# The preparation of a state-space scan, done by direction and half instead of by channel chunk

## The chip, the core and the metric

The kernel runs on one NeuronCore of a Trainium2 chip. The core has five engines that run side by side, each through its own list of instructions in order: TensorE (PE, matrix products, with its weight loads shown apart as PEld), VectorE (DVE, element by element), ScalarE (ACT, functions of one input), GpSimd (POOL, here two-input products), and SyncE (SP, which here issues most transfers). On-chip data lies in SBUF; matrix products land in PSUM[...]. The metric is the device time in microseconds (us) of one execution.

## What is computed

The input x has 8 images of 384 channels and 32 x 32 pixels, which are a sequence of L = 1024 places. Layer 0 normalizes it over the channels, runs a selective state-space model (Mamba) forward and backward over the sequence, adds a gated 3 x 3 depthwise convolution, and adds all to x. Layer 1 is a causal attention with 6 heads and a feed-forward part with sign weights and 8-bit scaling. The part that matters here, cut from the reference:

```python
xz = jnp.einsum('blc,ec->ble', x, in_proj_w)
u, z = jnp.split(xz, 2, axis=-1)
uc = conv_general_dilated(u...)                      # causal, 4 taps per channel
u = silu(uc + conv1d_b)
x_dbl = jnp.einsum('blc,ec->ble', u, x_proj_w)
dt, Bm, Cm = jnp.split(x_dbl, [dt_rank, dt_rank + D_STATE], axis=-1)
delta = softplus(einsum('blr,dr->bld', dt, dt_proj_w) + dt_proj_b)
h = exp(delta * A) * h + (delta * u) * Bm            # one step of the scan, 16 states
y = sum_n(h * Cm) + u * D_param
y = y * silu(z)
...
fwd = mamba(x_flat); bwd = flip(mamba(flip(x_flat)))
g = (fwd + bwd) * scale_mod
x = x + res_scale * (g + sigmoid(conv3x3(x_norm) + dw_b) * x_norm)
```

Everything is float32 except the causal mask. The forward and the backward scan use the same weights.

## The kernel before, in words

Channels lie on the 128 partitions, so C = 384 is three chunks c; places lie along a row, in two halves h of HB = 512 columns. The kernel is written as lists of small steps, each with an estimated weight in us. A scheduler orders the instructions that the steps record, and the tile pools decide which buffer each takes: `mid` has 10 buffers of 1024 columns, `big` 6 of 3 x 1024 columns, and PSUM has 8 banks (`da` 2, `s` 2, `pt` 2, `y` 1, `av` 1).

**The recurrence.** The scans of one batch are 96 units (`Unit`): four parts (direction d and half h, `PARTS` = forward first half, forward second, backward second, backward first), three chunks c, eight pairs of states n. A unit is: POOL multiplies `ud` (delta times u) by a broadcast row of B (`s_first`, L578); ACT makes exp(delta A) into PSUM (L591) and DVE scans, twice (L596, `s_scan`); POOL multiplies by a row of C (L602); PE transposes the product and adds it up in PSUM (L610, `s_sum`). After the last unit of a chunk and half, `s_gate` adds u D and multiplies by silu(z). A unit's first multiply is recorded two units ahead of its scan, and its loads (`ud`, `dl`, rows `bc`) four units ahead. The part's rows of B and C are read from DRAM.

**The preparation, `before_scan`.** It makes all of this for a batch ahead of its scans. It loads x, normalizes both halves (L330), and then goes by chunk: `in_proj` makes u (`up`) and z of both halves (L337, L344); `conv` makes the four-tap convolution for each direction and half, one tap on ACT (L353) and three on DVE (L363); `gates` applies Silu, makes the image convolution `local` (L374 and eight taps L384 on DVE), and spills x and z; the sum of the u of both directions (L428) and u itself go to DRAM. `project` multiplies u of the chunk by the x_proj weights; the chunks' contributions are added up in SBUF, in `xd`, by DVE (L488). After the third chunk, the rows of B and C are spilled and `delta` runs for every chunk, direction and half: it reloads u, one matmul (L508), four ACT functions (L511 to L514) and four DVE operations (L515 to L518), and spills delta (`dl`) and `ud`. [...]

**The order of the stages.** Batches go in the order 0, 1, 2, 3, 5, 6, 4, 7. The preparation of batch 0 runs first, but for its `gates` for z and the image (`later`). Then the first scans (`first`, the 96 units of batch 0) run with a list `beside` them: these gates, the preparations of batches 1, 2 and 3, and the binarization of the feed-forward weights. After that, the units of the next batch run beside the attention of the batch before (`attention`), and beside its feed-forward part (`feed_forward`, batches 0 to 4) together with the preparation of a batch three further on. The attention of the last batch has nothing beside it.

The steps are laid into one another by `spread_over`, in proportion to their weights; the lists are put together in these lines:

```python
before_scan(ORDER[0], ("s", "pt"), begin, beside)
run(begin)
beside += steps_of(before_scan, ORDER[1], ("s", "pt"))
...
run(first, beside)
```

Of the kernel before, what the change touches and what calls it, by code (L numbers as in the profile page):

```python
# [17 lines left out]
P = 128  # L18
# [35 lines left out]
def kernel(  # L54
# [251 lines left out]
    def before_scan(b, tags, emit, later=None):  # L306

        st = {}
        turns = itertools.cycle(tags)

# [3 lines left out]
        @emit  # L314
        def _():

            st["xn"] = btile(f"xn_{b}")
            load(st["xn"], x[b].rearrange("(c p) l -> p c l", p=P))
            st["xd"] = mtile(f"xd_{b}")

        for h in range(NH):

            @emit
            def _(h=h):
                sqs = squares(st["xn"], h, f"n0_{b}")
                ms = mean_of(lambda c: sqs[c], f"ms_{b}_{h}")
                rstd_of(ms, 0)
                for c in range(NC):
                    xc = st["xn"][:, c, half(h)]
                    nc.vector.scalar_tensor_tensor(  # L330
                        xc, xc, vec[:, c, V_NORM : V_NORM + 1], ms, ALU.mult, ALU.mult
                    )

        def in_proj(c, i, h):
            mp = bank_of(f"in_{b}_{c}_{i}_{h}")
            for k in range(NC):
                nc.tensor.matmul(  # L337
                    out=mp,
                    lhsT=st["win", c][:, k, i, :],
                    rhs=st["xn"][:, k, half(h)],  # L340
                    start=(k == 0),
                    stop=(k == NC - 1),
                )
            nc.scalar.copy(st["up" if i == 0 else "z", c][:, half(h)], mp)  # L344

        def conv(c, d, h):

            acc = bank_of(f"u{d}_{b}_{c}_{h}")
            up = st["up", c]
            for s in range(DCONV):  # L350
# [14 lines left out]
                st["u", d, c][:, half(h)], acc, AF.Identity, bias=vec[:, c, V_CB : V_CB + 1]  # L365
# [28 lines left out]
        def weights_of(c):  # L394
            w = mtile(f"win_{b}_{c}", NC * 2 * P).rearrange("p (k i e) -> p k i e", k=NC, i=2)
            for i in range(2):
                load(
                    w[:, :, i, :],
                    w_in[:, i * C + c * P : i * C + (c + 1) * P].rearrange("(k p) e -> p k e", p=P),
                )  # L400
            st["win", c] = w

        emit(lambda: weights_of(0))
        for c in range(NC):

            @emit
            def _(c=c):
                st["up", c] = mtile(f"up_{b}_{c}")
                st["z", c] = mtile(f"z_{b}_{c}")
                for d in range(2):  # L410
                    st["u", d, c] = mtile(f"u{d}_{b}_{c}")
                if c + 1 < NC:
                    weights_of(c + 1)

            for i in range(2):
                for h in range(NH):
                    emit(lambda c=c, i=i, h=h: in_proj(c, i, h), 2.6)
            for d in range(2):
                for h in range(NH):
                    emit(lambda c=c, d=d, h=h: conv(c, d, h), 3.0)  # L420

            def silus(ts):
                for t in ts:
                    pin(nc.scalar.activation(t, t, AF.Silu))

            def sum_of_us(c=c):
                usum = mtile(f"us_{b}_{c}")
                nc.vector.tensor_tensor(usum, st["u", 0, c], st["u", 1, c], ALU.add)  # L428
                spill((b, "us", c), usum, f"sus_{b}_{c}")
                for d in range(2):  # L430
                    spill((b, "u", d, c), st["u", d, c], f"su_{d}_{b}_{c}")


            def gates(c=c, silus=silus, sum_of_us=sum_of_us):
                st["xc"] = mtile(f"xc_{b}_{c}")
                load(st["xc"], x[b, chunk(c), :])
                accs = [local(c, h) for h in range(NH)]
                with tc.high_priority(offset=60):
                    us = [st["u", 0, c], st["u", 1, c]] if later is None else []
                    silus(us + [st["z", c]])  # L440
                    for h in range(NH):
                        pin(
                            nc.scalar.activation(
                                accs[h], accs[h], AF.Tanh, scale=0.5, bias=dwbh[:, c : c + 1]
                            )
                        )
                    pin(nc.scalar.preload_act_table_set(LOG_EXP))
                for h in range(NH):
                    acc, xc = accs[h], st["xc"][:, half(h)]
                    nc.vector.scalar_tensor_tensor(  # L450
                        acc, acc, 1.0, st["xn"][:, c, half(h)], ALU.add, ALU.mult
                    )
                    nc.vector.scalar_tensor_tensor(xc, acc, rsh, xc, ALU.mult, ALU.add)
                spill((b, "t", c), st["xc"], f"st_{b}_{c}")
                spill((b, "z", c), st["z", c], f"sz_{b}_{c}")
                if later is None:
                    sum_of_us()

            def gates_of_us(c=c, silus=silus, sum_of_us=sum_of_us):
                with tc.high_priority(offset=60):  # L460
                    silus([st["u", 0, c], st["u", 1, c]])
                    pin(nc.scalar.preload_act_table_set(LOG_EXP))
                sum_of_us()

            if later is None:
                emit(gates, 14.0)
            else:
                emit(gates_of_us, 4.0)
                later(gates, 10.0)


            for h in range(NH):

                def project(c=c, h=h):
                    xp = bank_of(f"xp_{b}_{c}_{h}")
                    for d in range(2):
                        nc.tensor.matmul(
                            out=xp[d * DW : (d + 1) * DW, :],
                            lhsT=wx[:, c, :],
                            rhs=st["u", d, c][:, half(h)],  # L480
                            start=True,
                            stop=True,
                        )
                    xd = st["xd"][:, half(h)]
                    if c == 0:
                        nc.scalar.activation(xd, xp, AF.Identity, bias=onerow)
                    else:
                        nc.vector.tensor_tensor(xd, xd, xp, ALU.add)  # L488

                emit(project)  # L490

        @emit
        def _():
            for d in range(2):
                rows = dram.tile([2 * NS, L], F32, name=f"rows{d}_{b}", tag=f"rows{d}")
                nc.sync.dma_start(out=rows, in_=st["xd"][d * DW + BC0 : (d + 1) * DW, :])
                spilled[b, "rows", d] = rows
# [3 lines left out]
        def delta(c, d, h):  # L501
            ew = mtile(f"ew{d}_{b}_{c}_{h}").rearrange("p (i l) -> p i l", i=2)
            du = mtile(f"du{d}_{b}_{c}_{h}").rearrange("p (i l) -> p i l", i=2)
            e, w, dl, u = ew[:, 0, :], ew[:, 1, :], du[:, 0, :], du[:, 1, :]
            load(u, spilled[b, "u", d, c][:, half(h)])
            dp = bank_of(f"dp{d}_{b}_{c}_{h}")
            r = slice(d * DW, d * DW + RANK + 1)
            nc.tensor.matmul(  # L508
                out=dp, lhsT=wdt[r, chunk(c)], rhs=st["xd"][r, half(h)], start=True, stop=True
# [6 lines left out]
            nc.vector.scalar_tensor_tensor(dp, w, 1.0, e, ALU.subtract, ALU.subtract)  # L516
            nc.vector.tensor_tensor(dl, dl, dp, ALU.subtract)
            nc.vector.tensor_tensor(u, u, dl, ALU.mult)  # L518
            for i, what in enumerate(("dl", "ud")):
                t = dram.tile([P, HB], F32, name=f"s{what}_{d}_{b}_{c}_{h}", tag=f"sp_{what}_{d}_{c}_{h}")  # L520
                nc.sync.dma_start(out=t, in_=du[:, i, :])
                spilled[b, what, d, c, h] = t

        for c in range(NC):
            for d, h in PARTS:
                emit(lambda c=c, d=d, h=h: delta(c, d, h), 3.0)
# [39 lines left out]
    def s_row(u, i):  # L566

        if not u.asks:
            return
        r = sp.tile([P, 2, HB], F32, name=f"bc{i}_{u.name}", tag=f"bc{i}", bufs=4)  # L570
        rows = spilled[u.b, "rows", u.d][i * NS + u.n : i * NS + u.n + 2, half(u.h)]
        load(r, rows.partition_broadcast(P))
        sst["bc", i, u.b, u.part, u.n] = r
# [57 lines left out]
    def s_gate(u):  # L631
# [6 lines left out]
        for what in ("us", "z"):  # L638
            t = sp.tile([P, HB], F32, name=f"{what}h_{u.name}", tag=what, bufs=1)
            load(t, spilled[b, what, c][:, half(h)])  # L640
# [451 lines left out]
    def steps_of(stage, *args):  # L1092
        out = Steps()
        stage(*args, out)
        return out
# [92 lines left out]
```

## Time and profile before

| | |
|---|---|
| time, median of 3 runs | 5227.8 us (5223.77 to 5229.38) |
| span of the profiled execution | 5226.4 us |
| PE busy | 4198.9 us (80%) |
| POOL busy | 3680.7 us (70%) |
| DVE busy | 3630.7 us (69%) |
| ACT busy | 2738.5 us (52%) |
| DMA, bytes moved | 696.35 MB, mean 133 GB/s |

How to read it: a busy engine is busy over the whole span on average, while the stages have different limits, so a stage must be looked at by itself. A group of instructions is named by line, engine, operation and tiles (out<-in); then come its count, its busy time, the mean of one in ns, the idle time of its engine just before it, and what ended that. The two multiplies of the recurrence, with their form:

```profile
L578 POOL TENSOR_TENSOR g<-ud,bc 128x1024 f32<-128x1024 f32 x768 | 1834.5, 2389 | 730.6 <-PE y L610 579.9
L602 POOL TENSOR_TENSOR g<-g,bc 128x1024 f32<-128x1024 f32 x768 | 1819.8, 2370 | 277.6 <-DVE g L596 215.5
```

They are 768 units of two multiplies of some 2.4 us, nearly all of POOL's work.

### The profile page before, as it was taken

The numbers are of one execution on the slowest core, as the hardware profiler recorded it, in microseconds if no ns is written. First come the engines' busy times: TensorE is split into PE (matmuls) and PEld (weight loads), VectorE is DVE, ScalarE is ACT, GpSimd is POOL, SyncE is SP. The second block draws the span as 40 slices with busy tenths as digits, with TensorE's granted clock in tenths as the row PEclk, the third lists the DMA queues.
The fourth block names the chain that finished last, engine by engine and source line by source line (L and its number), as shares of the span: only waits on it lengthen the run. The fifth ranks groups of instructions, "written<-read, shape, count | busy, mean of one in ns | idle before, by whom it ended". The sixth has DMA issues, their size and how long they took to land.

```text
span 5226.4 us, 50586 instructions
## 1 busy us (share of the span) xinstructions
PE 4198.9 (80%) x16554; PEld 2222.6 (43%) x16554; DVE 3630.7 (69%) x4313; ACT 2738.5 (52%) x4934; POOL 3680.7 (70%) x1932
## 2 busy tenths in 40 slices
PE   5455667888878888788887888978888888988799
PEld 2233333444434444444443444434444444544444
DVE  6998998667776667876677856678766655565522
ACT  4665564555644556545556445565464454463334
POOL 0477777887679776787776788677888877787600
PEclk7667677889988899888898889988999989999899
DMA  6544545324463234543244632335433234224200
GB/s 228 210 164 156 184 166 196 109 84 149 143 205 105 91 110 161 169 158 119 97 139 133 213 123 91 108 128 201 141 119 130 89 101 158 85 77 151 83 30 25
DMA packets 365007, 696.35 MB, mean 133 GB/s; under 512 B 30104, under 2 KB 88904, under 8 KB 364744
## 3 DMA queue, kind: packets, MB, share of 16 engines
q1 hardware_dynamic: 355232, 676.97, 38.3%
q10 hardware_dynamic: 9512, 16.15, 0.9%
q8 instruction: 131, 2.15, 0.2%
q14 instruction: 132, 1.08, 0.1%
HBM read 527.33 MB, written 165.68 MB: 133 GB/s over the span
## 4 chain that ended last, share of the span: by engine, by line
POOL 35%; PE 21%; issue 16%; DVE 15%; ACT 4%; DMA 1%; POOLq 0%; SPq 0%; DVEq 0%; ACTq 0%
POOL g L578 18%; POOL g L602 17%; DVE g L596 6%; PE y L610 3%; PE qp L715 3%; PE yp L1015 2%; PE av L854 2%; PE s L770 2%; PE ap L911 2%; DVE loc L384 2%; PE pt L842 1%; DVE dp L516 1%; DVE u L363 1%; PE hp L970 1%; DVE du L518 1%
## 5 line engine op out<-in xcount | busy, mean ns | idle before, releaser
L578 POOL TENSOR_TENSOR g<-ud,bc 128x1024 f32<-128x1024 f32 x768 | 1834.5, 2389 | 730.6 <-PE y L610 579.9
L602 POOL TENSOR_TENSOR g<-g,bc 128x1024 f32<-128x1024 f32 x768 | 1819.8, 2370 | 277.6 <-DVE g L596 215.5
L591 ACT ACTIVATE da<-dl,amat 128x512 f32<-128x512 f32 x1536 | 1057.5, 691 | 1572.1 <-DVE g L596 1530.2
L610 PE MATMUL y<-ident,g 128*128 128x128 f32 x6144 | 969.2, 307 | 403.1 <-POOL g L602 337.6
L596 DVE TENSOR_TENSOR_SCAN g<-da,carry,g 128x512 f32<-128x512 f32 x768 | 954.9, 1271 | 460.2 <-POOL g L578 413.2
L596 DVE TENSOR_TENSOR_SCAN g<-da,g 128x512 f32<-128x512 f32 x768 | 906.5, 1209 | 508.5 <-POOL g L578 483.0
L610 PEld LDWEIGHTS y<-ident,g 128*128 128x128 f32 x6144 | 798.8, 158 | 837.3 <-POOL g L602 504.1
L770 PE MATMUL s<-k,q 64*128 64x512 f32 (+3 forms) x1152 | 469.9, 606 | 166.0 <-ACT pr L790 143.7
L789 DVE TENSOR_REDUCE nm<-s 128x1 f32<-128x512 f32 (+3 forms) x576 | 300.4, 545 | 251.0 <-PE s L779 182.5
L790 ACT ACTIVATE pr<-s,nm 128x512 f32<-128x512 f32 (+3 forms) x576 | 329.4, 575 | 149.5 <-DVE nm L789 148.4
L854 PE MATMUL av<-ptn,v 128*64 128x512 f32 (+3 forms) x1152 | 376.5, 556 | 24.8 <-DVE o L866 24.3
L970 PE MATMUL hp<-t,w 128*128 128x512 f32 x720 | 339.4, 615 | 33.2 <-ACT h L978 10.6
L842 PE MATMUL pt<-ident,pr 128*128 128x128 f32 x1728 | 312.3, 302 | 46.8 <-ACT ptn L844 24.3
L337 PE MATMUL in<-xn,win 128*128 128x512 f32 x576 | 301.2, 665 | 57.2 <-DVE xn L330 16.6
L1015 PE MATMUL yp<-h,w 128*128 128x512 f32 x720 | 330.5, 617 | 10.9 <-DMA w<-w2s 10.9
L844 ACT COPY ptn<-pt 128x512 f32<-128x512 f32 (+3 forms) x576 | 261.8, 480 | 128.8 <-PE pt L842 127.5
L770 PEld LDWEIGHTS s<-k,q 64*128 64x128 f32 x1152 | 163.3, 207 | 332.6 <-ACT pr L790 214.1
L842 PEld LDWEIGHTS pt<-ident,pr 128*128 128x128 f32 x1728 | 209.0, 152 | 180.7 <-ACT ptn L844 82.0
L715 PE MATMUL qp<-t,wqk 128*128 128x512 f32 x576 | 268.0, 616 | 22.0 <-DVE t L301 16.5
L601 POOL COPY carry<-g 128x2 f32<-128x2 f32 x384 | 84.4, 220 | 255.5 <-DVE g L596 255.5
L384 DVE SCALAR_TENSOR_TENSOR loc<-xn,vec,loc 128x496 f32<-128x496 f32 (+3 forms) x384 | 254.6, 721 | 4.3 <-ACT loc L374 4.0
L363 DVE SCALAR_TENSOR_TENSOR u<-up,vec,u 128x512 f32<-128x512 f32 (+3 forms) x288 | 201.5, 743 | 30.8 <-ACT u L353 30.4
(156 smaller groups left out, 4695.0 us busy)
## 6 DMA issues: line engine op xcount, KB each, us to landing
bc<-rows SPq DMA_DIRECT2D x512, 512.0 KB, 4.0
dl<-sdl SPq DMA_DIRECT2D x160, 256.0 KB, 2.8
ud<-sud SPq DMA_DIRECT2D x160, 256.0 KB, 2.7
t<-st SPq DMA_DIRECT2D x63, 512.0 KB, 5.1
su<-u SPq DMA_DIRECT2D x48, 512.0 KB, 5.2
du<-su SPq DMA_DIRECT2D x96, 256.0 KB, 4.5
sdl<-du SPq DMA_DIRECT2D x96, 256.0 KB, 2.7
sud<-du SPq DMA_DIRECT2D x96, 256.0 KB, 2.4
```

Of the source, the lines that this page charges most:

```text
L384: nc.vector.scalar_tensor_tensor(to, src[:, i0 + di : i1 + di, j0 + dj : j1 + dj], vec[:, c, V_DW + k : V_DW + k + 1], to, ALU.mult, ALU.add,)
L578: pin(nc.gpsimd.tensor_tensor(g, ud, sst["bc", 0, u.b, u.part, u.n], ALU.mult))
L591: nc.scalar.activation(da, sst["dl", u.b, u.c, u.part], AF.Exp, scale=amat[:, u.c, n : n + 1])
L596: nc.vector.tensor_tensor_scan(gi[:, ::step], da[:, ::step], gi[:, ::step], first, ALU.mult, ALU.add)
L602: pin(nc.gpsimd.tensor_tensor(g, g, sst["bc", 1, u.b, u.part, u.n], ALU.mult))
L610: nc.tensor.matmul(out=y[:, j, :], lhsT=g[:, i, chunk(j)], rhs=ident, is_transpose=True, start=(u.opens and i == 0 and j == 0), stop=(u.cl ...
L715: nc.tensor.matmul(out=qp, lhsT=st["wqk"][:, c, o : o + P], rhs=st["xn"][:, c, half(h)], start=(c == 0), stop=(c == NC - 1),)
L770: nc.tensor.matmul(out=ss[e][:, : k1 - k0], lhsT=st["q"][rows_of(e), c, chunk(qi)], rhs=st["k"][rows_of(e), c, k0:k1], start=True, stop=(k ...
L842: nc.tensor.transpose(pt[:, chunk(i)], pr[:, e, chunk(j % QT)], ident)
L854: nc.tensor.matmul(out=av[rows_of(e), cols], lhsT=st["v"][:, j, hd * HD : (hd + 1) * HD], rhs=st["ptn", j, e][:, cols], start=(j % QT == 0 ...
L970: nc.tensor.matmul(out=hp, lhsT=st["w1"][:, c, chunk(m % 2)], rhs=st["xn"][:, c, half(h)], start=(c == 0), stop=(c == NC - 1),)
L1015: nc.tensor.matmul(out=yp, lhsT=st["w2", k // 6][:, k % 6, :], rhs=st["h", k // NC][:, k % NC, half(h)], start=(k == 0), stop=(k == NF - 1),)
```

## The change

The preparation goes by part (direction and half) instead of by chunk. A part does the convolution for its three chunks, their Silu, its projection and its deltas. Parts 1 to 3 each also take one chunk of z and of the image gate. For batch 0 only the first half's norm and u and part 0 run ahead of the first recurrence; the second half and parts 1 to 3 go into the list beside the first scans. The parts stand in the order in which the units need them.

- `project` of a part adds up its three chunks in one PSUM bank, and one ACT instruction takes the result to SBUF; the DVE adds (L488) are gone. Rows are spilled by direction and half.
- u stays in SBUF from `conv` to `delta` (one tile `du`, with delta in its other half). The first direction to come to a half spills its u; the second reloads that and adds its own (the sum of both, 512 columns).
- In the preparations of the first four batches in order (those with `w_all`), `delta` keeps two intermediate values in PSUM banks, so that no DVE operation of the four has two SBUF inputs, and copies the final delta to SBUF with ACT.
- The weights of `in_proj` are loaded once for the first four batches, in one `big` buffer; for the other four, each chunk of u or z loads its own just before its first use.
- x is loaded in two halves.

```diff
+            st["xn"] = btile(f"xn_{b}")
+            for h in range(NH):
+                load(
+                    st["xn"][:, :, half(h)],
+                    x[b].rearrange("(c p) l -> p c l", p=P)[:, :, half(h)],
+                )
...
         def in_proj(c, i, h):
+            if ("uz"[i], c) not in st:
+                st["uz"[i], c] = mtile(f"{('up', 'z')[i]}_{b}_{c}")
+                o = i * C + c * P
+                if w_all is None:
+                    w = mtile(f"win_{b}_{c}_{i}", NC * P).rearrange("p (k e) -> p k e", k=NC)
+                    load(w, w_in[:, o : o + P].rearrange("(k p) e -> p k e", p=P))
...
+        def project(d, h):
+            xp = bank_of(f"xp{d}_{b}_{h}")
+            r = slice(d * DW, (d + 1) * DW)
+            for c in range(NC):
+                nc.tensor.matmul(
+                    out=xp[r, :],
+                    lhsT=wx[:, c, :],
+                    rhs=st["du", c][:, 1, :],
+                    start=(c == 0),
+                    stop=(c == NC - 1),
+                )
+            nc.scalar.activation(st["xd"][r, :], xp[r, :], AF.Identity, bias=onerow[r, :])
...
         def delta(c, d, h):
...
-            load(u, spilled[b, "u", d, c][:, half(h)])
+            other = dl if w_all is None else w
+            if (b, "u", 1 - d, c, h) in spilled:
+                load(other, spilled[b, "u", 1 - d, c, h])
+                nc.vector.tensor_tensor(other, other, u, ALU.add)
+                keep("us", c, 0, h, other)
+            else:
+                keep("u", c, d, h, u)
...
+            if w_all is not None:
+                w = bank_of(f"w{d}_{b}_{c}_{h}")
...
-            nc.vector.scalar_tensor_tensor(dp, w, 1.0, e, ALU.subtract, ALU.subtract)
-            nc.vector.tensor_tensor(dl, dl, dp, ALU.subtract)
-            nc.vector.tensor_tensor(u, u, dl, ALU.mult)
+            if w_all is None:
+                nc.vector.scalar_tensor_tensor(dp, w, 1.0, e, ALU.subtract, ALU.subtract)
+                nc.vector.tensor_tensor(dl, dl, dp, ALU.subtract)
+                nc.vector.tensor_tensor(e, u, dl, ALU.mult)
+            else:
+                nc.vector.scalar_tensor_tensor(w, w, 1.0, e, ALU.subtract, ALU.subtract)
+                nc.vector.tensor_tensor(dp, dl, w, ALU.subtract)
+                nc.vector.tensor_tensor(e, u, dp, ALU.mult)
+                nc.scalar.copy(dl, dp)
...
+        def part_of(part, to):
+            d, h = PARTS[part]
+            zc = part - 1 if part else None
+            for c in range(NC):
+                to(lambda c=c: conv(c, d, h), 3.0)
+            if zc is not None:
+                for k in range(NH):
+                    to(lambda k=k: in_proj(zc, 1, k), 2.6)
+            to(lambda: gates(zc), 5.0 if zc is None else 12.0)
+            to(lambda: project(d, h))
+            for c in range(NC):
+                to(lambda c=c: delta(c, d, h), 3.0)
...
-    before_scan(ORDER[0], ("s", "pt"), begin, beside)
+    w_all = weights("w_in", w_in)
+    before_scan(ORDER[0], ("s", "pt"), begin, beside, w_all)
```

## The prediction

> **What bounds the kernel now.** I read first the busy time of each engine by stage, cut where GpSimd (POOL) starts its first multiply, where the scan of the first batch ends (its 96 units), and where the last scan ends. The columns are stretch, length, then busy time and instructions of PE, PE weight loads, VectorE (DVE), ScalarE (ACT) and POOL, the PE clock, and DMA.
>
> ```profile
> 0.00:144.00 144.00, 71.36 (x134) 27.42 (x134) 93.45 (x140) 68.53 (x94) 9.20 (x15) 0.71 0.68 239
> 144.00:836.00 692.00, 411.06 (x1230) 216.58 (x1230) 639.83 (x759) 426.31 (x635) 465.64 (x241) 0.67 0.52 177
> 836.00:949.00 113.00, 98.23 (x342) 55.41 (x342) 77.09 (x80) 46.56 (x75) 108.68 (x68) 0.90 0.46 155
> 949.00:4945.00 3996.00, 3360.55 (x13874) 1805.99 (x13873) 2743.05 (x3188) 2096.79 (x3871) 3097.18 (x1610) 0.90 0.38 128
> 4945.00:5226.00 281.00, 257.72 (x978) 117.20 (x976) 77.27 (x149) 100.33 (x261) 0.00 (x0) 0.92 0.10 38
> ```
>
> Four regimes: an opening of 144 us without recurrence; a first stage of 692 us in which DVE is busy 639.8 (92%), since the preparation of three more batches lies beside the first scan; one quarter of 113 us in which POOL is full (108.7); then a long mix with PE at 84%, POOL 78%, DVE 69%; a tail without POOL.
>
> Then POOL's order of time at the opening: the first recurrence multiply waits 132 us.
>
> ```profile
> 133.90 7.86 POOL L578 TENSOR_TENSOR g<-ud,bc 128x1024 f32<-128x1024 f32 x3 [131.99 <-DMA sdl<-du]
> ```
>
> Then DVE's waits in the first stage (who waited for whom: us, times, longest). These four are 43.5 of its 52 us of idle time, so DVE sets this stage.
>
> ```profile
> DVE g L596 <- ACT da L591: 16.8, 8, 4.1
> DVE g L596 <- POOL g L578: 12.2, 11, 2.5
> DVE yt L629 <- PE y L610: 7.3, 3, 3.5
> DVE du L515 <- ACT du L514: 7.2, 7, 2.3
> ```
>
> Last the groups of the delta step in that stage (count, busy us, mean ns), and the same L516 and L518 before POOL runs.
>
> ```profile
> L516 DVE SCALAR_TENSOR_TENSOR dp<-ew 128x512 f32<-128x512 f32 x42 | 63.8, 1530 | 0.2
> L518 DVE TENSOR_TENSOR du<-du 128x512 f32<-128x512 f32 x42 | 43.7, 1050 | 0.1
> L517 DVE TENSOR_TENSOR du<-du,dp 128x512 f32<-128x512 f32 x42 | 27.8, 671 | 0.2
> L515 DVE SCALAR_TENSOR_TENSOR du<-dp,du 128x512 f32<-128x512 f32 x41 | 27.4, 677 | 7.2 <-ACT du L514 7.2
> ...
> L488 DVE TENSOR_TENSOR xd<-xd,xp 128x512 f32<-128x512 f32 x12 | 7.8, 666 | 0.0
> ```
> ```profile
> L516 DVE SCALAR_TENSOR_TENSOR dp<-ew 128x512 f32<-128x512 f32 x4 | 2.7, 693 | 0.0
> L518 DVE TENSOR_TENSOR du<-du 128x512 f32<-128x512 f32 x3 | 2.0, 682 | 0.0
> ```
>
> The same instruction costs 0.69 us while POOL rests and 1.05 to 1.53 us beside it, and only where both inputs lie in SBUF; L515 and L517, with one input in PSUM, stay at 0.67.
>
> [...]
>
> **The change part by part.**
>
> *Deltas in PSUM (first four batches).* Of four DVE operations two lose their second SBUF input. Over the whole kernel's mean prices (0.677, 1.386, 0.670, 1.198 = 3.93 us) against 0.677+0.677+0.67+0.67 = 2.69: 1.24 us each. In the instruction order 47 deltas stand before the end of the first 96 units, now 45: 184.8 us become 121.4, so -63.4 on DVE. It adds a copy on ACT (about 0.58 us, the price of L344) for each of 48: 28 us on an engine that is busy 426 of 692; hidden.
>
> *Projections in PSUM.* Four adds L488 of 0.67 us a batch go: 16 in this stretch, -10.7. The 12 matmuls a batch stay 12. Two more ACT identities a batch, hidden.
>
> *Sum of both directions by halves.* 12 sums of 1.52 us become 21 of 1.2 by that point (two SBUF inputs at 512 columns, taken as L518): +7.0. Each new sum waits for a reload of the other direction's u, in front of the scans.
>
> *Moved behind unit 96 by the order:* 15 image taps L384 and a few gates, -13.7, which return in the next quarter.
>
> Sum: before the end of unit 96 the order puts 804.6 us of DVE work at these prices, after the change 724.2. Prices count the overlap of neighbours twice: in the stage 698 us of prices were 639.8 us busy, a factor 0.916.
>
> *A quarter ahead of the first scan.* The order puts 103 us of DVE work ahead of the first scan before, 42.6 after (9 conv taps in place of 36, 10 delta operations for 19, the rest binarization). The first multiply, from durations in this trace: w1 lands at 26.4 as before; three reductions and three scalings of xn on DVE, 4.2 -> 30.6; three matmuls, a copy and a scale, 3.5 -> 34.1; nine taps with five reductions between, 9 -> 43; bias, table load, three Silus, table load, 5.2 -> 48.3; the sign of w1 stands ahead on ACT, 2.8 -> 51.1; xd, matmul, two deltas on ACT, 5.8 -> 56.8; six DVE operations 3.7 -> 60.5; write and reload of ud (2.4 and 2.7 us to landing, 0.8 to issue), and one us behind other issues -> 67. It was 133.9. Two scans and their wait put unit 0 at 72, before 144.
>
> *First stage.* (724.2 - 43.8) x 0.916 = 623 us busy, 52 us of the idle time seen now, and 15 us that I add for the 24 reloads: some stand on SP's queue behind row loads that wait for POOL, so a sum may find its data 1 to 5 us late (256 KB land in 2.7 to 4.5). I take 15, the ends are 0 and 24 x 3 = 72. So unit 96 ends at 72 + 690 = 762, against 836: -74.
>
> *The next quarter.* It gets 21 us more DVE work (77 of 113 busy now, POOL 109): it fits beside POOL. +4.
>
> *Later batches.* DVE work is even there (adds -10.7, sums +3 and what was moved). Three things differ. Table loads: 159 in the order against 130, 10 of the 29 in the first stage; 19 x 1.283 = 24 us on ACT at 52%: I take +5 of 0 to 24. Weights: a batch had three chunks, loaded one ahead; now six loads stand right before their use, 24 in all, behind which PE holds the transposes that free g for POOL. A load takes 4.9 us; PE waited 10.9 us for these in the whole run before. Ends 0 and 24 x 4 = 96; PE has 16% of slack and SP often issues ahead, so +15. Against it, the 12 deltas stood in a block at the end of each preparation: in four windows of 100 us (from 1500, 2200, 2900 and 3600) DVE is busy 83, 88, 89, 88 and POOL only 74, 68, 68, 69 instead of 78. A perfectly even spread could give 100 x (1 - 70/78), about 10 us each, 40 in all; half is -20. Net 0. The tail is unchanged, as are PE's matmul counts and their places between the transposes.
>
> Sum: -74 + 4 + 0 = -70, so 5228 - 70 = 5158 us.
>
> **The rivals.** (A) *A wait takes the place*: the reloaded u stalls DVE at nearly every sum of the first stage, 72 in place of 15: -13, about 5215. For it: strict order and SP's waits on POOL (bc loads are behind it). Against: DVE waits for no DMA in this stage today, and the order puts several operations between load and sum. (B) *Later batches pay*: all 24 weight loads exposed (+96) and all table loads (+24) without the smoothing: 5228 - 70 + 120 = 5278; with half, 5220 to 5245. Slower or at the edge. For it: POOL's wait for y of PE is already 580 us, the largest of its waits. Against: PE's wait for w2 loads, placed just as closely, is 11 us. (C) *More than the sum*: no reload stall (-15) and the whole smoothing without the costs (-40): about 5105. For it: the four windows above. Against: gates with 16 image taps remain as lumps.
>
> **How the numbers follow.** Main case 0.61, C 0.20, A 0.10, B 0.09. Faster by over 0.2% (below 5217): main, C, half of A, 0.86; same 0.05; slower 0.09. The range takes in the ends of C and A, 5100 to 5225; outside lie most of B and what would go beyond C, together under 2 in 10.
>
> **What would show it.** Right: first multiply at 60 to 75 us; DVE still over 88% busy up to unit 96, which ends near 762; the two delta operations at about 0.68 us in the first four batches and still 1.2 to 1.4 in the others; no DVE adds for xd; the span from unit 96 to the end within 20 us of 4390. Wrong: a multiply at 67 but unit 96 still past 810 (A; DVE waits for ew loads), or PE waits for the weights of tens of us and a longer span after unit 96 (B).

## The result and the profile after

| | before | after |
|---|---|---|
| time, median | 5225.8 us (5217.9 to 5229.4) | 5295.2 us (5272.6 to 5304.1) |
| ratio, with its 95% interval | | 1.0128 [1.0091, 1.0165] |
| span of the profiled execution | 5226.4 us | 5285.6 us |
| POOL's last multiply ends | 4945.0 us | 5006.8 us |
| DMA, bytes moved | 696.35 MB | 667.66 MB |

The change makes the kernel slower by 1.3%, some 67 us, where 70 us less were forecast. The stages of after, cut as before where the first unit, the first 96 units and the last unit end (stretch, length, then busy time and instructions of PE, its weight loads, DVE, ACT, POOL; then PE's granted clock, the share of DMA time and GB/s):

```profile
0.00:91.00 91.00, 30.34 (x46) 10.96 (x46) 40.96 (x69) 31.22 (x45) 8.30 (x15) 0.72 0.67 243
91.00:806.00 715.00, 444.54 (x1296) 229.62 (x1296) 628.94 (x800) 499.63 (x758) 469.36 (x243) 0.69 0.48 162
806.00:949.00 143.00, 115.24 (x395) 63.38 (x396) 96.18 (x113) 66.14 (x105) 114.95 (x71) 0.87 0.43 149
949.00:5007.00 4058.00, 3393.07 (x13844) 1823.06 (x13843) 2757.35 (x3180) 2117.76 (x3905) 3087.75 (x1605) 0.89 0.36 123
5007.00:5285.00 278.00, 255.20 (x977) 116.85 (x975) 77.29 (x149) 100.11 (x261) 0.00 (x0) 0.92 0.10 39
```

The first two rows won: they took 836 us and take 806. The third, 24 units, takes 143 us; before took 120.3 us for the same 24 units (the prediction's row of 113 us ends two units short of them). The fourth is long. To compare kernels without stage borders that move, here is the time at which POOL ends its second multiply of a unit, read from the trace (us; only e1, e3, e9 and e13, explained below, beside the two). Each column is one execution; four executions of after differ by up to 31 us.

| unit | before | after | e1 | e3 | e9 | e13 |
|---|---|---|---|---|---|---|
| 0 | 147.1 | 93.7 | 92.5 | 93.2 | 92.2 | 147.2 |
| 24 | 345.9 | 284.2 | 282.3 | 283.5 | 282.4 | 346.4 |
| 96 | 838.6 | 806.0 | 807.5 | 805.5 | 803.7 | 840.7 |
| 144 | 1099.5 | 1097.8 | 1087.3 | 1083.2 | 1080.9 | 1099.8 |
| 336 | 2318.7 | 2342.4 | 2309.7 | 2319.9 | 2287.1 | 2309.6 |
| 552 | 3694.9 | 3733.6 | 3692.9 | 3717.5 | 3667.0 | 3692.0 |
| 648 | 4221.8 | 4290.7 | 4219.7 | 4276.0 | 4219.8 | 4228.7 |
| 767 | 4945.0 | 5006.8 | 4942.9 | 4988.7 | 4939.7 | 4948.6 |

After is 33 us ahead at unit 96, 2 us at unit 144, and 69 us behind at unit 648; from there to the end it no longer changes by more than 10 us. So the lead goes between units 96 and 144, and the loss against before builds up beside the preparations of the four later batches and just behind them.

The recurrence multiplies show the same from POOL's side (count, busy, mean ns, then idle time just before and what ended it):

```profile
L580 POOL TENSOR_TENSOR g<-ud,bc 128x1024 f32<-128x1024 f32 x768 | 1829.9, 2383 | 884.6 <-PE y L612 772.7 <-DMA ud<-sud 79.6 <-DVE nm L791 13.8
L604 POOL TENSOR_TENSOR g<-g,bc 128x1024 f32<-128x1024 f32 x768 | 1821.9, 2372 | 234.8 <-DVE g L598 141.5 <-issue 53.0 <-DMA bc<-rows 9.0
```

A multiply costs what it did (2389 and 2370 ns before); the wait for PE's transposes, `y`, grew from 579.9 to 772.7 us. PE's own waits between 1100 and 4940 us say for whom PE stood (us, times, longest):

```profile
...
PE y L612 <- POOL g L604: 87.2, 25, 24.3
PE yb L651 <- ACT yt L627: 52.5, 18, 20.9
PE in L352 <- DMA win<-in_w_in: 45.4, 8, 20.1
...
PE y L612 <- ACT yt L627: 41.3, 7, 21.7
```

The first line shown isn't part of the loss: before has 136.4 us there. The third is new in size: before, PE waited 6.7 us for in_proj's weights in the same stretch. The second and fourth are waits for ACT and grew from 13.6 and 17.2 us. One of these waits, on PE and then on ACT (start, us, instruction, idle before it):

```profile
1401.92 1.12 PE L651 MATMUL yb<-ident,yt 128*128 128x128 f32 x4 [20.88 <-ACT yt L627]
```
```profile
1387.53 1.28 ACT L997 ACT_TABLE_LOAD   x1
1388.83 2.86 ACT L997 ACTIVATE h<-h,qs_h 128x3072 f32<-128x3072 f32 x1
1391.70 1.28 ACT L998 ACT_TABLE_LOAD   x1
...
1398.67 0.69 ACT L380 ACTIVATE du<-u,vec 128x512 f32<-128x512 f32 x1 [0.81 <-ACT h L997]
...
1401.29 0.58 ACT L627 COPY yt<-y 128x512 f32<-128x512 f32 x1
```

A copy of 0.58 us that PE needs stands in ACT's queue behind the deltas' functions, two Gelus with their table loads, and the convolution. Two theories were made from these lines: that the later preparations fill the ten `mid` buffers (up, du, xd, ew and a weight tile), and that their weights are fetched too late. A third, about the weights of the step lists, came from the clock column, below.

### The profile page after: what moved, and what is told of

It reads as the page before. It is cut to its first block, busy times and chain, and to the rows that moved or that the text cites. A ratio compares the mean times of both kernels' runs of the same rounds, so it can differ in the third digit from the quotient of the medians.

```text
span 5285.6 us, 50709 instructions
## 1 busy us (share of the span) xinstructions
PE 4238.4 (80%) x16554; PEld 2243.9 (42%) x16554; DVE 3600.7 (68%) x4308; ACT 2814.9 (53%) x5072; POOL 3680.4 (70%) x1932
## 2 busy tenths in 40 slices
DMA packets 290785, 667.66 MB, mean 126 GB/s; under 512 B 29736, under 2 KB 79320, under 8 KB 290520
## 4 chain that ended last, share of the span: by engine, by line
POOL 37%; PE 22%; issue 18%; DVE 13%; ACT 6%; DMA 4%; SPq 0%; POOLq 0%; ACTq 0%; DVEq 0%
POOL g L580 18%; POOL g L604 18%; DVE g L598 5%; PE y L612 3%; PE av L856 2%; PE s L772 2%; PE yp L1017 2%; PE qp L717 2%; DVE u L379 2%; PE hp L972 2%; PE pt L844 2%; PE ap L913 1%; PE in L352 1%; PE op L687 1%; ACT da L593 1%
## 5 line engine op out<-in xcount | busy, mean ns | idle before, releaser
L580 POOL TENSOR_TENSOR g<-ud,bc 128x1024 f32<-128x1024 f32 x768 | 1829.9, 2383 | 884.6 <-PE y L612 772.7
L612 PEld LDWEIGHTS y<-ident,g 128*128 128x128 f32 x6144 | 798.6, 158 | 805.5 <-issue 382.4
L772 PE MATMUL s<-k,q 64*128 64x512 f32 (+3 forms) x1152 | 481.7, 627 | 142.6 <-ACT pr L792 125.5
L972 PEld LDWEIGHTS hp<-t,w 128*128 128x128 f32 x720 | 136.9, 199 | 199.8 <-issue 145.4
L1017 PEld LDWEIGHTS yp<-h,w 128*128 128x128 f32 x720 | 138.5, 196 | 194.9 <-issue 165.8
```

The source lines that it names most:

```text
L580: pin(nc.gpsimd.tensor_tensor(g, ud, sst["bc", 0, u.b, u.part, u.n], ALU.mult))
L612: nc.tensor.matmul(out=y[:, j, :], lhsT=g[:, i, chunk(j)], rhs=ident, is_transpose=True, start=(u.opens and i == 0 and j == 0), stop=(u.cl ...
L772: nc.tensor.matmul(out=ss[e][:, : k1 - k0], lhsT=st["q"][rows_of(e), c, chunk(qi)], rhs=st["k"][rows_of(e), c, k0:k1], start=True, stop=(k ...
L972: nc.tensor.matmul(out=hp, lhsT=st["w1"][:, c, chunk(m % 2)], rhs=st["xn"][:, c, half(h)], start=(c == 0), stop=(c == NC - 1),)
L1017: nc.tensor.matmul(out=yp, lhsT=st["w2", k // 6][:, k % 6, :], rhs=st["h", k // NC][:, k % NC, half(h)], start=(k == 0), stop=(k == NF - 1),)
```

## The experiments

Each is one edit of a named kernel. Ratios are to the kernel before on the same chip, with the 95% interval; a hundredth of a per cent is half a us.

**Which half of the change loses (e1, e2).** e1 leaves the first four batches by part and prepares the later four as before; e2 is the reverse.

```diff
-            fed = spread_over(fed, steps_of(before_scan, later.pop(0), ("pt", "pt", "av")))
+            fed = spread_over(fed, steps_of(before_scan_old, later.pop(0), ("pt", "pt", "av")))
```

> The four later batches are prepared as before the change, the first four by part. Theory (the later batches pay: the changed kernel loses 62 us between unit 144 and the end, in the stretches beside which a batch is prepared): the loss after unit 144 goes away, within 15 us, so about 5225 to 5235 us. Rival (the loss after unit 144 comes from how the first stage leaves the queues, or from the clock): it stays near 5290.

> The first four batches are prepared as before the change, the four later ones by part. Theory (later batches pay 62 us by themselves, the first stage nets nothing by unit 144): 5280 to 5295 us, with unit 144 at 1099 as before. Rival (first stage to blame): about 5230.

e1: 5217.9 us, ratio 0.9968 [0.9956, 0.9980]. e2: 5290.3 us, 1.0101 [1.0082, 1.0119]. The early part gains 0.3%, the later part alone costs 1.0%. In e1 PE waits 6.4 us for in_proj's weights. So what makes the kernel slower than before is in the later four batches, where the forecast had put a net 0. The early part alone, for which it had put -70 us, brings some 17. The two ratios don't add up to the 1.0128 of after, which was measured on another chip from four runs and has a wide interval; so what the later part costs is known only as 1.0 to 1.6%.

**Weights one use ahead (e3).** In the later batches of the changed kernel, a chunk's weights are loaded while the chunk before is used, and those of z at the start of a part.

```diff
-                    load(w, w_in[:, o : o + P].rearrange("(k p) e -> p k e", p=P))
-                    st["win"] = w
+                    st["win"] = st.pop(("win", c, i))
+                    if i == 0 and c + 1 < NC:
+                        fetch(c + 1, 0)
```

> The changed kernel, but each chunk of in_proj weights of the four later batches is loaded one use ahead (u) or at the start of its part (z). Theory (PE stands before a matmul whose weights have just been asked for, 45 us in all against 7, with the transposes that free g behind it): 30 to 50 us of the 62 come back, about 5245 to 5265, and PE waits under 12 us for win. Rival (the 10 mid buffers are short, so whatever is asked for early waits for a buffer instead): no gain or a loss, 5285 to 5305, and the waits move to other loads or to ACT.

5269.4 us, 1.0061 [1.0040, 1.0081]. PE's waits for these weights, 45.4 us in after, are gone from the list; the same matmuls now wait 50.1 us in four pieces behind ACT, so the wait in part only changed its cause, as the rival had it. Still about half of the loss comes back; the rest was open.

**The deltas' intermediates in SBUF (e4).** The first four batches use the delta step of the later ones: no PSUM banks, no copy on ACT.

```diff
         def delta(c, d, h):
+            psum = False
...
-            if w_all is not None:
+            if psum:
```

> The changed kernel, but the deltas of the first four batches keep their intermediate values in SBUF, as before, with no copy on ACT. If PSUM deltas save DVE time that sets the first stage (63 us by count): unit 96 ends 40 to 60 us later, at 845 to 865, and the time is about 5330. If the copy on ACT and its place in ACT's queue give the saving back: within 10 us of the changed kernel.

Unit 96 ends at 859.3 us, not 806.0: 53 us, so PSUM deltas are worth in the first stage about what their working said (63.4 times 0.916 is 58). The end is another thing: 5308.9 us, 1.0143 [1.0118, 1.0167], beside 1.0128 [1.0091, 1.0165] for after. In the two profiles the 53 us at unit 96 are 21 at unit 144 and 17 at the last unit. Most of a gain in the first stage doesn't arrive at the end.

**Are the `mid` buffers short (e5, e6, e7)?** e5 and e6 are e1 in which each later preparation holds one or three `mid` buffers from start to end, unused. Both take buffers from the old form of the later preparation; e7 gives one back in the new form: it is e3 with xd in the free half of a weight tile, one buffer less for each part.

```diff
+            st["held"] = [mtile(f"held{k}_{b}") for k in range(3)]
+            for t in st["held"]:
+                nc.scalar.copy(t[:, 0:1], onecol)
...
+        before_scan_old(b, tags, emit)
```
```diff
-            st["xd"] = mtile(f"xd{d}_{b}_{h}", HB)
+            st["xd"] = mtile(f"xd{d}_{b}_{h}", HB) if w_all is not None else st["beside"]
```

> The kernel of e1 (first four batches by part, later four as before, 5218 us), and each later preparation holds one `mid` buffer from its start to its end, unused. Theory M (the later batches by part lose because up, du, xd, ew and a weight tile fill the ten `mid` buffers, so that ACT stands for a du buffer with the scan behind it): 5 to 20 us above e1, 5223 to 5238. Rival T (they lose because the deltas' Exp and Ln now meet the Gelu of the feed-forward part in ACT's queue, whatever the buffers): within 8 us of e1.

> As e5_hold_one with three buffers held. Theory M: 35 to 80 us above e1, 5253 to 5298, with waits of 10 us and more of PE for ACT beside the feed-forward parts. Rival T: within 10 us of e1, 5208 to 5228.

> e3_fetch_ahead (5269 us), and in the later batches xd of a part lies in the free half of the `mid` buffer of its last weights, so that a part needs one buffer less. Theory M: 15 to 40 us below e3, 5229 to 5254, and the three waits of PE behind ACT L386 (18.4, 16.1, 14.7 us in e3) fall under 6. Rival T: within 8 us of e3 and the waits stay.

e5: 5220.4 us, 0.9971 [0.9961, 0.9981]. e6: 5215.6 us, 0.9957 [0.9943, 0.9972]. With three of ten buffers taken away the kernel isn't slower at all. e7: 5288.5 us, 1.0092 [1.0071, 1.0112], no gain over e3, and PE's four waits behind the convolution's ACT instruction stayed at 53.0 us in sum (e3 50.1). The buffer theory falls, although the trace's long ACT waits had suggested it.

**The stand of DVE in the opening (e8).** e1, with the binarization of w2 one batch later in the list.

```diff
-    beside += steps_of(binarize, w2, w2s, NF, C, 8, "w2")
-    for b in ORDER[2 : 1 + ahead]:
-        beside += steps_of(before_scan, b, ("s", "pt"), w_all=w_all)
+    beside += steps_of(before_scan, ORDER[2], ("s", "pt"), w_all=w_all)
+    beside += steps_of(binarize, w2, w2s, NF, C, 8, "w2")
+    beside += steps_of(before_scan, ORDER[3], ("s", "pt"), w_all=w_all)
```

> The kernel of e1 with the binarization of w2 after the preparation of the third batch in the list, not before it, so that DVE does not stand for w2's load ahead of the first scan. If the opening's missing 19 us are this stall: unit 0 ends 10 to 16 us before e1's 92.5. If the lead is then kept through the next quarters: 5202 to 5210. Rival (a lead at unit 0 is given back by unit 144, since the work merely moves): within 6 us of e1's 5218.

Unit 0 ends at 86.5 us (e1 92.5), less than expected; unit 96 at 811.9 (e1 807.5). 5225.0 us, 0.9975 [0.9962, 0.9988], not different from e1. Six us at unit 0 were gone by unit 96.

**The weights of the lists (e9 to e12).** The steps carry estimated weights, and the units are laid beside them in proportion. The change cut the sum of a later preparation from 180.2 to 161.7, since fewer steps are listed, not since they take less time. With JOINT = 0.6 a batch is then 531.1 in the planner's list and not 542.2. e9 is e3, and e11 is after, with the old sum; e10 is e1 with the new sum; e12 is e1 with 198.0.

```diff
+            prepared = steps_of(before_scan, later.pop(0), ("pt", "pt", "av"))
+            grown = 180.2 / sum(us for _, us in prepared)
-            fed = spread_over(fed, steps_of(before_scan, later.pop(0), ("pt", "pt", "av")))
+            fed = spread_over(fed, Steps((f, grown * us) for f, us in prepared))
```

> e3_fetch_ahead (5269 us) with the weights of the later preparations' steps multiplied so that a preparation's list adds up to 180.2 as before, not 161.7. Theory P (the lighter lists move units away from the stretches with a preparation and into the attention, which is PE's): 25 to 50 us below e3, 5219 to 5244, and units 552 to 648 back from 558 us to about 527. Rival W (what the later preparations contain: weights fetched in line, Exp and Ln beside Gelu): within 8 us of e3.

> The kernel of e1 (later preparations as before, 5218 us) with the weights of their steps multiplied so that a list adds up to 161.7 in place of 180.2; nothing else changes. Theory P: 25 to 50 us above e1, 5243 to 5268, units 552 to 648 at about 555 us and not 527. Rival W: within 8 us of e1.

> The changed kernel (5295 us) with the later lists' weights back to 180.2 in sum, the weights of in_proj fetched right before use as in the change. Theory P: 25 to 50 us below it, 5245 to 5270. Rival W: within 8 us of it. Its difference to e9 is then the price of the late fetch alone.

> The kernel of e1 with the later lists' weights up to 198.0 in sum. If the old sum was well tuned by its own place, theory P gives 5218 to 5250 (past the best point); if more units beside the preparations still help, 5195 to 5215. Rival W: within 8 us of e1.

| | list sum | weights fetched | time | ratio to before |
|---|---|---|---|---|
| after | 161.7 | in line | 5295.2 | 1.0128 [1.0091, 1.0165] |
| e11 | 180.2 | in line | 5244.1 | 1.0027 [1.0017, 1.0038] |
| e3 | 161.7 | ahead | 5269.4 | 1.0061 [1.0040, 1.0081] |
| e9 | 180.2 | ahead | 5216.7 | 0.9974 [0.9964, 0.9983] |
| e1 | 180.2 | as before | 5217.9 | 0.9968 [0.9956, 0.9980] |
| e10 | 161.7 | as before | 5250.5 | 1.0040 [1.0028, 1.0052] |
| e12 | 198.0 | as before | 5219.8 | 0.9984 [0.9974, 0.9995] |

The old sum brings 1.0% (53 us) with weights in line, 0.9% (45 us) with weights ahead, and the new sum alone costs e1 0.7% (38 us). Fetching ahead brings 0.5 to 0.7% (28 to 35 us). Both together undo the whole loss. A mere number in a list, with no operation added or taken away, is the larger part of it. The old sum isn't sharp as a best value: 198.0 (e12) gives nearly the same as 180.2 (e1). Nor is the sum all that counts: e14 and e15 below keep it in the later lists, change other weights, and lose 20 to 35 us against e9. That this plan is good and most changes of it lose is a rival to "the sum must be kept" which these runs don't exclude.

What such a number does is seen only in part. The planner paces 576 units evenly over the lists of six batches, four with a preparation and two of an attention alone (weight 306.5). So an attention gets 576 x 306.5/(4 x 542.2 + 2 x 306.5) = 63.5 units beside it with the old sum and 64.5 with the new; each later preparation with its feed-forward part gets 1.5 less. A scheduler then puts all the queues in another order. The profile shows what came of it between unit 144 and unit 552, for e3 and then for e9:

```profile
1083.00:3717.50 2634.50, 2186.66 (x8434) 1158.77 (x8431) 1895.21 (x2171) 1426.37 (x2466) 1965.18 (x1033) 0.88 0.40 132
```
```profile
1081.00:3667.00 2586.00, 2158.85 (x8399) 1145.25 (x8396) 1879.90 (x2162) 1423.76 (x2459) 1966.39 (x1031) 0.89 0.40 133
```

Of the 48.5 us, PE is busy 28 less and idle 21 less, with nearly the same matmuls and a higher granted clock (the column ahead of the DMA share). Units 552 to 648, where no preparation runs any more, show that alone: e1, after, e10, e9 and e11 in this order.

```profile
3693.00:4220.00 527.00, 454.81 (x2142) 252.84 (x2142) 340.88 (x409) 268.91 (x578) 454.18 (x241) 0.93 0.34 111
```
```profile
3734.00:4291.00 557.00, 479.64 (x2148) 266.09 (x2147) 343.63 (x405) 269.47 (x576) 453.46 (x241) 0.88 0.31 105
```
```profile
3697.50:4248.00 550.50, 471.04 (x2146) 263.62 (x2144) 342.85 (x406) 268.74 (x576) 453.37 (x241) 0.90 0.32 107
```
```profile
3667.00:4220.00 553.00, 480.99 (x2156) 265.26 (x2154) 344.27 (x413) 269.86 (x577) 454.04 (x242) 0.89 0.33 113
```
```profile
3705.00:4241.00 536.00, 460.74 (x2155) 257.54 (x2154) 343.26 (x413) 268.72 (x577) 453.40 (x241) 0.92 0.34 117
```

Some 2150 matmuls each, PE idle for 72 to 80 us in each, POOL's work the same; the granted clock is 0.93, 0.88, 0.90, 0.89, 0.92, and the length follows. So against e1 after, e10 and e9 lose 24 to 30 us in a stretch that holds none of the changed code. The expectation of e9 was that the old sum brings this back; in e9 it did not, in e11 most of it came. e9 has its lead before this stretch (28 us against before at unit 552) and gives it up there. Yet the traces of e9, e11, e13 and e14 show the same instructions in the same order on PE, DVE, ACT and POOL there (but for one matmul record), and they took 552.8, 536.2, 536.7 and 549.2 us. So the order of the work alone doesn't set the length.

What the clock does can be read one step further. In the traces of before, after, e1, e3 and e9 it has two values only, 1.00 and 0.50, in pieces that are, but for the last of a trace, multiples of 3.4 us. After at 4014 us, in stretches of that length:

```profile
4010.10:4013.50 3.40, 3.40 (x23) 2.12 (x21) 2.99 (x3) 2.44 (x6) 3.25 (x2) 1.00 0.27 102
4013.50:4016.90 3.40, 2.13 (x10) 0.89 (x9) 2.83 (x3) 2.21 (x7) 3.40 (x3) 1.00 0.21 57
4016.90:4020.30 3.40, 3.40 (x9) 1.46 (x10) 2.30 (x4) 1.79 (x6) 3.40 (x2) 0.50 0.09 31
...
4030.60:4034.00 3.40, 3.40 (x14) 2.41 (x13) 1.92 (x4) 1.27 (x5) 1.19 (x1) 0.50 0.31 62
4034.00:4037.40 3.40, 3.30 (x24) 2.08 (x22) 3.40 (x4) 3.01 (x7) 3.40 (x2) 1.00 1.03 418
```

In the second stretch PE stands for 1.3 us, in waits for ACT; then the clock is halved for 17 us. Two of av's matmuls of 256 columns took 0.65 us ahead of the drop and 1.12 us behind it; over the whole of after, a transpose of `y` took 273 ns in the median at the full clock and 421 ns at the halved one. What stands ahead of a change can be counted in the traces of before and after, by PE's busy share of the 3.4 us ahead of it (by the profile, which models the ends of matmuls). Ahead of the 151 and 159 drops it is 0.32 and 0.34 in the median and at most 0.92, and 0.63 in the second row above. Ahead of the 150 and 158 returns to the full clock it is 1.00 in the median and never below 0.81. In the other stretches at the full clock it is 1.00 in the median and at least 0.43, in the other ones at the halved clock 0.58 in the median. So a drop mostly follows a stretch in which PE stands for much of the time, and a return one in which it hardly stands. But the shares overlap, and after the drop above four stretches in which PE never stands pass without a return; the rule itself was not shown. Between units 144 and 767 the clock is halved for 768 us in before, 785 in e1, 795 in e9, 843 in after and 857 in e3. From e1 to after that is 58 us more at the halved clock; if half of that is lost, an estimate, it is 29 us of work, and PE is busy 27.6 us more. On this reading a wait of PE would be paid twice: by itself, and by the slow stretch after it, and the second part would depend on how short waits fall together. That would also let the same order give different lengths, as in e9 and e11. It is the author's estimate, which fits the traces, but no run tests it: through which waits, in which windows, the lists' weights act stays open.

**What is left (e13, e14, e15).** e13 is e9 with the first four batches as before the change. e14 is e9 with an empty step at the end of the list beside the first scans, so that the fourth preparation is done earlier; e15 is e9 with the steps with image taps at weight 20.

```diff
+    beside(lambda: None, 0.05 * sum(us for _, us in beside))
     run(first, beside)
```
```diff
-            to(lambda: gates(zc), 5.0 if zc is None else 12.0)
+            to(lambda: gates(zc), 5.0 if zc is None else 20.0)
```

> e9_pace_back (5217 us) with the first four batches as before the change, so the later part alone, with weights fetched ahead and the old sum of weights. If the two faults were all that the later part cost, it equals the kernel before within 10 us (ratio 0.998 to 1.002). Rival (deltas in four blocks and four groups of Silu cost something themselves): 15 to 30 us above it, ratio 1.003 to 1.006.

> e9_pace_back with an empty step of 5% weight at the end of the list beside the first scans, so that the fourth preparation is done before unit 96. Lump theory (POOL stands 17 us once after unit 96, since DVE has a block of image taps and deltas ahead of a scan): unit 96 ends 5 to 15 us later than e9's 804, the 17 us stall is gone, unit 144 ends up to 12 us sooner than 1081 and the end too. Rival (the same work only moves): unit 144 and the end within 6 us of e9.

> e9_pace_back with the weight of the steps with image taps at 20, not 12 (the later lists still add up to 180.2), so that more scans stand around each lump of 16 taps. Lump theory: less waiting of POOL for DVE, 5 to 20 us below e9's 5217. Rival: within 6 us, or slower by the units that then stand in the lumps' place.

e13: 5232.9 us, 0.9996 [0.9983, 1.0009]: with both faults mended the later part in sum neither costs nor brings anything that can be told from 0. So the deltas in four blocks, which now meet the Gelus in ACT's queue (the rival in the expectations of e5 to e7), have no net price, though PE's four long waits behind ACT are still in e9's list (50.9 us). e14: 5242.3 us, 1.0012 [0.9998, 1.0025]; unit 96 ends at 827.3 us, 24 later than in e9, and 21 of that are still there at the last unit. e15: 5256.2 us, 1.0040 [1.0025, 1.0055]. Both expectations rest on this line of after, POOL's small copy that waits for a scan behind a block of image taps and deltas:

```profile
825.61 0.19 POOL L603 COPY carry<-g 128x2 f32<-128x2 f32 x1 [17.30 <-DVE g L598]
```

e14 did not pay for its later unit 96; between 780 and 1100 us POOL still waits up to 16.5 us at once for DVE and 20.0 for PE. So the lump theory found no support. Where the lead between units 96 and 144 goes was not settled.

Faster than before, with an interval below 1, are e1, e5, e6, e8 and e9, by 0.25 to 0.43%, and e12 by 0.16%. The intervals of the first five overlap, so none of them is the best.

## Why the prediction was wrong, step by step

Forecast were 5228 - 70 us; the change costs 67. Some 50 us of this miss are the first stage and the quarter behind it (e1: 17 won of 70), the rest is the step "Later batches, net 0".

*The first multiply at 67 us*: right in kind, too large in size. It came forward by 52 us, not 67:

```profile
81.50 6.95 POOL L580 TENSOR_TENSOR g<-ud,bc 128x1024 f32<-128x1024 f32 x3 [79.60 <-DMA ud<-sud]
```

The two first deltas are done on DVE at 66.6 us, later than the 60.5 of the sum, and the write and reload took the rest. The first scan came still later, at 88.0, behind this on DVE:

```profile
84.73 2.17 DVE L224 TENSOR_REDUCE sums_w<-w 128x1 f32<-128x608 f32 x3 [12.09 <-DMA w<-in_w]
```

The step looked at DVE's work ahead of the scan, and not at a wait for the load of w2 that stands between in DVE's queue; with w2 later in the list, e8 gained 6 us. Unit 0's scans ended at 91, not 72.

*The first stage, 690 us long*: it took 715. Busy time was well worked out (629 us for 623), as were its parts. The two delta operations (L493, L495) cost 0.69 and 0.67 us where 1.53 and 1.05 were paid, there are no adds for xd, and the sums L472 took 1.0 us each for 1.2:

```profile
L493 DVE SCALAR_TENSOR_TENSOR w<-w,ew 128x512 f32<-128x512 f32 x42 | 28.9, 689 | 0.0
L495 DVE TENSOR_TENSOR ew<-du,dp 128x512 f32<-128x512 f32 x43 | 28.9, 672 | 0.0
...
L472 DVE TENSOR_TENSOR ew<-ew,du 128x512 f32<-128x512 f32 x21 | 20.9, 1005 | 8.7 <-DMA ew<-su 6.0 <-ACT da L593 2.4 <-issue 0.3
```

With both inputs in SBUF, in e4, the same two operations took 1428 and 965 ns in that stage, beside the same scans. The idle time was 86 us, not 67, and not from the reloads, which made DVE wait 6.0 us and not 15. DVE's waits in the stage:

```profile
DVE g L598 <- ACT da L593: 25.2, 11, 3.9
DVE du L487 <- ACT du L486: 16.9, 14, 2.9
DVE g L598 <- POOL g L580: 9.4, 5, 2.5
DVE loc L431 <- ACT loc L424: 9.4, 7, 3.0
DVE ew L472 <- DMA ew<-su: 6.0, 3, 3.1
```

Most are waits for ACT: it went to 499.6 of 715 us, and DVE's waits for its da and du grew from 24.0 to 42.1 us. "28 us on an engine that is busy 426 of 692; hidden" does not hold. In e4, which has no copies on ACT but slower deltas on DVE, DVE waits for du 0.3 us in place of 16.9, and is idle 72.5 us in all from unit 0 to unit 96. Its waits for da, 23.7 us, are there without the copies; their cause stays open. Unit 96 came at 806, not 762: 19 us from the opening, 6 busy, 19 idle.

*The next quarter, +4*: +23 (143.4 us for 120.3). DVE has 96 of 143 us of work there, which does fit beside POOL on average, as argued; but it doesn't come evenly: POOL waits 18.1 us for DVE there (17.3 at once, the line above) and 8.1 for PE, where it waited 2.5 us in all in before.

*Later batches, net 0*: this step turned a small gain into a loss. The second rival, that later batches pay, names the right place, but its 5278 us come close by luck: it has a lead of 70 us that never came, and +96 for the weight loads. Of its terms, the weight loads were +15 with ends 0 and 96; the pairs of runs give 28 to 35. The smoothing, -20, did not come, or was eaten by costs of the same size: in e13 all terms but the two faults sum to between -9 and +5 us. And one term was missing altogether: the weights of the listed steps, which set where the units lie, 38 to 53 us. The numbers stand in the diff (`3.0`, `2.6`, `12.0`); adding them up would have shown that a batch's list had become shorter, and the prediction never did. Its sentence that PE's "places between the transposes" are unchanged was wrong: already between units 552 and 648 the traces show PE's instructions in another order in after than in before. The table loads did come (159 for 130 in the traces, 1283 ns each; in both traces one stands wherever ACT goes from a Silu or Gelu to an Exp or Ln, or back), but no run put a price on them alone.

*The first rival*, stalls on reloaded u, is refuted by the 6.0 us, though SP waited 316 us for POOL in that stage (309 in before). *The third*, more than the sum, had nothing behind it.

## What to carry to other kernels

Where a planner lays streams into one another by estimated weights, splitting or merging steps changes the plan: add up each list before and after. Here three pairs of runs lost 38 to 53 us by a sum that had changed unseen; keep it at first, so that one thing changes at a time, and tune it on purpose. Price every load that moves next to its use on the engine that waits for it, even where a like load looks cheap. A gain in a stage with its own limit counts only as far as it is still there some hundred us later; here 33 us at unit 96 were 2 to 19 at unit 144.

## What the hardware showed that was not expected

The same stretch of some 2150 matmuls (units 552 to 648) took 527 us at a granted clock of 0.93 and 557 at 0.88, with PE's idle time within 5 us. Five kernels with the old lists of the later batches (before, e1, e5, e6, e8) had 526.7 to 529.9 us there, and six with the sum of 161.7 (after, e2, e3, e4, e7, e10) had 550.3 to 558.5, though within a group they reach unit 552 at times that differ by up to 15 and 59 us. So the slow windows go in part with the order of the work. But e9, e11, e13 and e14 run one and the same order there and took 536.2 to 552.8 us, with the clock halved for 75 to 126 us; so the moment, or what the engines bring along, counts too. Which it is was not tested. Over units 144 to 767 half of the 53 us between e1 and after is PE busier with the same work (3240.8 and 3268.4 us), and only the other half is waiting. A forecast in durations of the old trace, as this one, doesn't see the first half.
